# Two graph layers on one core: layer norm by sums, short reciprocals, and a second feed-forward product by seven block products

## The chip, the cores and the metric

The kernel runs on one core of a Trainium2 chip. The metric is the device time in microseconds. The engines are TensorE (PE in the profile, with its weight loads as PEld), VectorE (DVE), ScalarE (ACT), GpSimd (POOL) and SyncE (SP), which issues the transfers.

## The reference

There are 64 graphs of 256 nodes with 256 features, and an adjacency matrix for each. Two layers follow each other.

```
# layer 0
h = gat(gat(x, adj, W1, a1), adj, W2, a2)       # two graph attention layers
h = layernorm(x + h) * g_ln1 + b_ln1
ff = relu(h @ w_ff1 + b_ff1) @ w_ff2 + b_ff2    # 256 -> 1024 -> 256
x = layernorm(h + ff) * g_ln2 + b_ln2
# layer 1
attn = softmax(q k^T / sqrt(32)), 8 heads       # q, k: x @ Wq + bq, x @ Wk + bk
out = sum over r of (attn * (adj == r)) @ (x @ Wv[r] + bv[r])
x = layernorm(x + out @ Wo + bo) * g1 + beta1
ff = gelu(x @ W1 + b1) @ W2 + b2                # 256 -> 1024 -> 256
x = layernorm(x + ff) * g2 + beta2
```

All is float32.

## The kernel before

The graphs are taken in 32 pairs. `whole_way(pair)` (L943) is a Python generator that takes a pair through four stages: `gat_layers` (L515), `feed_forward` for layer 0 (L658), `attention` (L724), and `feed_forward` again for layer 1. The rows of a pair stand in one tile `x` with four row blocks, two for each graph; four such tiles exist.

The order of the instructions on each engine is written by a planner, `run` (L213), when the program is built. It has a clock for each engine, a cost in microseconds for each piece of work (`put`, L158; for matmuls `took`), the time at which a buffer or PSUM bank becomes free, and a rank. Four pairs are in flight at once, besides the generator that prepares the weights. At each step the planner takes the engine that can start earliest, and emits the first ready piece in order of rank and of the time at which it was ready. For TensorE the pair that holds the feed-forward stage stands behind the others; among the rest the oldest comes first. The order it finds is fixed by dependencies without semaphores, so each engine runs exactly this list.

*First product and projections.* The first feed-forward product and the query, key and value projections are done by seven block products instead of eight (`Second`, L344, and `Blocks`, L372): the operands' blocks are combined by additions, and the products are added up on VectorE (L392). The matmuls are at L681 (feed-forward), L754 and L759 (projections).

*Second product of a feed-forward stage.* It is done in the ordinary way. For each graph and each of its two row blocks, eight matmuls of 128 by 128 weights (the activations, `f`) and 256 moving columns (`w2`) add up in half a PSUM bank (L712), 32 matmuls for a pair. Then `add_rows` (L567) adds the bank to the rows of `x` on VectorE (L570), and `layernorm` (L572) follows for that graph, while the other graph's matmuls still run.

*Layer norm.* VectorE takes the statistics of each row block (L582, L583), adds epsilon and negates the mean (L584, L585). GpSimd raises to the power of -1/2 and multiplies by the mean (L588, L589). ScalarE normalises both row blocks (L593), VectorE multiplies by the gain and adds the shift (L598), each for both blocks in one instruction. In stages that go on, `transposed` (L608) turns the rows by VectorE, a store to memory and four gathers; in a few places at the start and the end (`hurried`, L604) TensorE transposes instead.

*Attention.* `scores(n)` (L788) is done for four combinations of graph and half of the heads. It takes four PSUM banks and multiplies queries and keys in tiles of 32 rows (L796). ScalarE takes the exponential of each head (L803), VectorE multiplies it by the adjacency (L807) and adds its halves (L811), one instruction for each head. `products(n)` (L818) multiplies with the values in tiles of 32 columns (L825) and adds the sums of the weights (L828). VectorE takes the reciprocal of those sums over 128 by 256 elements (L837), although each sum stands there 32 times, and multiplies (L838); ScalarE adds up sums and reciprocals for a check of their range (L835). The order is scores 0 and 1, products 0 and 1 together, scores 2 and 3, products 2 and 3 together.

The check of ranges decides at the end whether a second, general program has to run; with these inputs it doesn't.

Of the kernel before, what the change touches and what calls it, by code (L numbers as in the profile page):

```python
# [18 lines left out]
P = 128  # L19
# [7 lines left out]
HURRIED = 2  # L27
SLACK = 0.3
# [4 lines left out]
def two_layers(ctx: ExitStack, tc: tile.TileContext, t: dict, out: bass.AP, flag: bass.AP):  # L33
# [40 lines left out]

    rises = [const.tile([P, 2, 32], F32, name=f"rise{n}") for n in range(2)]
# [35 lines left out]
    a2, w1T = (work.tile([P, 512], F32, name="a", bufs=2 * HQ) for _ in range(2))  # L111
    junk = work.tile([P, N], F32, name="h", bufs=2 * HQ)
    w1T = w1T.rearrange("p (c m) -> p c m", c=KC)
# [27 lines left out]
    alone = {}  # L141
    free = {name: [0.0] * n for name, n in (("bank", 8), ("a", 2 * HQ), ("m", 2 * HQ), ("h", 2 * HQ), ("yb", 1), ("yT", 2), ("yTa", 1),
# [15 lines left out]
    def put(engine, us, emit, *events, rank=1, lag=0.2, kb=0, function=None, needs=None, frees=(), event=None):  # L158

        piece = {"engine": engine, "us": us, "emit": emit, "rank": rank, "lag": lag, "kb": kb, "function": function,
                 "needs": needs, "frees": frees, "event": event or Event(), "ready": 0.0, "missing": 0}
        for e in events:
            if e.time is None:
                piece["missing"] += 1
                e.then.append(piece)
            else:
                piece["ready"] = max(piece["ready"], e.time)
        if not piece["missing"]:  # L170
            waiting[engine].append(piece)
        return piece["event"]

# [39 lines left out]
    def run(besides, ways, together):  # L213
# [4 lines left out]
        together += 1  # L218
        while True:
# [23 lines left out]
            if engine == "tensor":  # L243
                sure = [n for at, n in times if at <= now - SLACK]
                g = going[min(sure, key=lambda n: (going[n][0] is besides, "ff" in (going[n][2] or ()) or alone.get("ff") is going[n][0], n))
# [11 lines left out]
            else:  # L257
                piece = waiting[engine].pop(min(able, key=lambda n: (waiting[engine][n]["rank"], waiting[engine][n]["ready"])))
# [68 lines left out]
    def first_weights(name, wide=None):  # L327
# [7 lines left out]
        return s  # L335

# [152 lines left out]
    def gat_weights(y, at, at_home, ratio, there, to, b):  # L489
# [16 lines left out]
        def scale():  # L506
            for j in range(2):
                k = 2 * b + j
                nc.scalar.activation(y[:, k, :at], y[:, k, :at], AF.Copy, scale=of["rs"][:, j:j + 1])  # L509

        there = put("vector", 1.03, lambda: weigh(0), *there, rank=b / 2, needs="e")
        there = put("vector", 1.11, lambda: weigh(1), there, rank=b / 2, frees=["rows"] * b)
        return of, put("scalar", 0.8, scale, there, rank=0)

    def gat_layers(pair, to, loads):  # L515
# [3 lines left out]
        def evacuated(to, k, wide, ps):  # L519
            return put("scalar", 0.4, lambda: nc.scalar.activation(to[:, k, :wide], ps[:, :wide], AF.Copy),  # L520
# [46 lines left out]
    def add_rows(y, p, b, *events):  # L567

        rows = y[:, of_graph(b), :].rearrange("p k d -> p (k d)")
        return put("vector", 0.6, lambda: nc.vector.tensor_tensor(rows, p, rows, ALU.add), *events, frees=["bank"])  # L570

    def layernorm(r, gb, b, *events):  # L572
        g, beta, _ = gb
        st = mv = rstd = less = None
        rows = [r[:, 2 * b + j, :] for j in range(2)]

        def statistics():
            nonlocal st, mv, rstd, less
            st, mv = small.tile([P, 2, 6], F32, name="st"), small.tile([P, 2, 2], F32, name="mv")
            rstd, less = small.tile([P, 2], F32, name="rstd"), small.tile([P, 2], F32, name="less")  # L580
            for j in range(2):
                nc.vector.bn_stats(st[:, j, :], rows[j])  # L582
                nc.vector.bn_aggr(mv[:, j, :], st[:, j, :])  # L583
            nc.vector.tensor_scalar(rstd, mv[:, :, 1], EPS, None, ALU.add)  # L584
            nc.vector.tensor_scalar(less, mv[:, :, 0], -1.0, None, ALU.mult)  # L585

        def root():
            nc.gpsimd.tensor_tensor(rstd, rstd, mhalf[:, :2], ALU.pow)  # L588
            nc.gpsimd.tensor_tensor(less, less, rstd, ALU.mult)  # L589

        def normalise():
            for j in range(2):
                nc.scalar.activation(rows[j], rows[j], AF.Identity, bias=less[:, j:j + 1], scale=rstd[:, j:j + 1])  # L593

        def scale():
            both = r[:, of_graph(b), :]
            for v, op in ((g, ALU.mult), (beta, ALU.add)):
                nc.vector.tensor_tensor(both, both, v.rearrange("p (k d) -> p k d", k=1).to_broadcast([P, 2, D]), op)  # L598

        there = put("vector", 1.22, statistics, *events)  # L600
        there = put("gpsimd", 1.2, root, there)
        return put("vector", 1.2, scale, put("scalar", 0.8, normalise, there))

# [54 lines left out]
    def feed_forward(y, normal, w, func, relieved, gb, pair, stage):  # L658

        w1, b1, w2 = w  # L660
# [3 lines left out]
        f, evacuated = [None] * NF, [[None] * NF for _ in range(2)]  # L664
# [5 lines left out]
        def slabs(t):  # L670

            rows, columns = [], (slice(0, N), slice(N, 2 * N))

            def begin():
                for c in range(2):
                    rows.append(work.tile([P, 2, 512], F32, name="ff", bufs=NF // 2))
                    for n in range(2):
                        f[t + n + c * half] = rows[c][:, n]
# [4 lines left out]
            def target(c, h):  # L683
                return rows[c][:, :, columns[h]]
# [715 lines left out]
```

## Time and profile before

| | |
|---|---|
| median of 3 runs | 3044.09 us (3042.1 to 3045.04) |
| the profiled execution, span | 3047.2 us |
| instructions in it | 52870 |
| PE busy | 2996.3 us |
| weight loads busy | 2452.5 us |
| DVE busy | 2556.8 us |
| ACT busy | 1752.5 us |
| POOL busy | 252.6 us |
| granted TensorE clock, mean | 0.995 |
| DMA queue of the data, share of 16 engines | 20.6% |

The profiled execution's own time is its span; it is 3.1 us above the median of the runs. Busy time is the time in which an engine had an instruction under way. Ends of matmuls are modelled, so their durations overlap; the distance between starts says more. In a timeline row stand the start, the length of the whole row, the engine, the line, the operation, the written and the read tiles, the tile of the array, the shape and the number of instructions; in brackets the idle time ahead of it and what ended it. In the rows of waits stand the total in microseconds, the number of times and the longest.

### The profile page before, as it was taken

The numbers are of one execution on the slowest core, as the hardware profiler recorded it, in microseconds if no ns is written. First come the engines' busy times: TensorE is split into PE (matmuls) and PEld (weight loads), VectorE is DVE, ScalarE is ACT, GpSimd is POOL, SyncE is SP. The second block draws the span as 40 slices with busy tenths as digits, with TensorE's granted clock in tenths as the row PEclk, the third lists the DMA queues.
The fourth block names the chain that finished last, engine by engine and source line by source line (L and its number), as shares of the span: only waits on it lengthen the run. The fifth ranks groups of instructions, "written<-read, shape, count | busy, mean of one in ns | idle before, by whom it ended". The sixth has DMA issues, their size and how long they took to land.

```text
span 3047.2 us, 52870 instructions
## 1 busy us (share of the span) xinstructions
PE 2996.3 (98%) x19146; PEld 2452.5 (80%) x19146; DVE 2556.8 (84%) x5993; ACT 1752.5 (58%) x4096; POOL 252.6 (8%) x518
## 2 busy tenths in 40 slices
PE   7999999999999999999999999999999999999998
PEld 6887788878888888888888888888888888788876
DVE  5888988788988888888889888889888898888875
ACT  4556666556556556555565565565555655555654
POOL 0100010001100001100001000011000011000100
PEclk8999999999999999999999999999999999999999
DMA  5211041212212222112222112221122221122100
GB/s 186 74 47 61 32 127 54 70 56 84 70 40 66 77 84 77 53 53 70 84 84 77 39 60 77 84 77 62 50 68 79 84 77 52 52 71 70 49 1 22
DMA packets 211147, 205.76 MB, mean 68 GB/s; under 512 B 22336, under 2 KB 170432, under 8 KB 210880
## 3 DMA queue, kind: packets, MB, share of 16 engines
q1 hardware_dynamic: 210464, 202.06, 20.6%
q8 instruction: 153, 2.51, 0.4%
q14 instruction: 114, 0.93, 0.1%
q10 hardware_dynamic: 416, 0.26, 0.0%
HBM read 137.51 MB, written 64.73 MB: 66 GB/s over the span
## 4 chain that ended last, share of the span: by engine, by line
PE 63%; DVE 25%; DMA 6%; ACT 2%; SPq 1%; issue 1%; POOL 0%; DVEq 0%; ACTq 0%; POOLq 0%
PE ps L712 21%; PE ps L681 15%; PE ps L825 5%; DVE x L598 4%; PE ps L759 4%; PE ps L754 4%; PE ps L544 3%; DVE h L837 3%; PE ps L796 3%; DMA home<-yb 3%; DVE st L582 2%; DVE m L807 2%; PE ps L557 2%; DMA rows<-row 2%; DVE ff L392 2%; PE ps L847 2%
## 5 line engine op out<-in xcount | busy, mean ns | idle before, releaser
L712 PE MATMUL ps<-w_L_gnn_w_ff,ff 128*128 128x256 f32 x2048 | 470.9, 381 | 0.0
L712 PE MATMUL ps<-w_L_gnn_W,ff 128*128 128x256 f32 x2048 | 456.1, 380 | 1.8 <-ACT ff L693 1.8
L593 ACT ACTIVATE x<-x,less,rstd 128x256 f32<-128x256 f32 x512 | 279.2, 596 | 294.8 <-POOL less L589 294.7
L712 PEld LDWEIGHTS ps<-w_L_gnn_w_ff,ff 128*128 128x128 f32 x2048 | 386.6, 190 | 61.5 <-issue 9.8
L712 PEld LDWEIGHTS ps<-w_L_gnn_W,ff 128*128 128x128 f32 x2048 | 388.2, 190 | 57.6 <-ACT ff L693 2.6
L588 POOL TENSOR_TENSOR rstd<-rstd,mhalf 128x2 f32<-128x2 f32 x256 | 198.3, 775 | 2765.7 <-DVE less L585 2638.0
L807 DVE TENSOR_TENSOR m<-a,adj 128x512 f32<-128x512 f32 x512 | 350.1, 684 | 57.9 <-ACT a L803 57.8
L803 ACT ACTIVATE a<-ps 128x512 f32<-128x512 f32 x512 | 268.0, 604 | 222.6 <-PE ps L796 222.5
L681 PE MATMUL ps<-yT,w_L_gnn_W1p 128*128 128x256 f32 x1280 | 315.2, 382 | 4.7 <-ACT ff L687 2.4
L392 DVE TENSOR_TENSOR ff<-ps,ff 128x512 f32<-128x512 f32 x384 | 262.7, 685 | 66.4 <-PE ps L681 58.3
L681 PE MATMUL ps<-yT,w_L_gnn_w_ff1p 128*128 128x256 f32 x1280 | 308.8, 382 | 6.8 <-ACT ff L687 5.9
L681 PEld LDWEIGHTS ps<-yT,w_L_gnn_w_ff1p 128*128 128x128 f32 x1280 | 240.6, 190 | 50.8 <-ACT ff L687 18.8
L687 ACT ACTIVATE ff<-ps 128x512 f32<-128x512 f32 x384 | 223.9, 590 | 98.4 <-PE ps L681 97.6
L681 PEld LDWEIGHTS ps<-yT,w_L_gnn_W1p 128*128 128x128 f32 x1280 | 240.2, 190 | 48.2 <-ACT ps L835 8.5
L837 DVE RECIPROCAL h<-ps 128x256 f32<-128x256 f32 x128 | 223.4, 1746 | 21.3 <-PE ps L828 20.9
L509 ACT ACTIVATE xw<-xw,rs 128x258 f32<-128x258 f32 (+1 forms) x256 | 115.9, 502 | 200.7 <-DVE rs L504 200.6
L693 ACT ACTIVATE ff<-ff,c_L_gnn_b_ff 128x256 f32<-128x256 f32 x384 | 171.6, 504 | 97.4 <-DVE ff L392 97.0
L693 ACT ACTIVATE ff<-ff,c_L_gnn_b 128x256 f32<-128x256 f32 x384 | 173.3, 501 | 85.0 <-DVE ff L392 83.8
L811 DVE TENSOR_TENSOR h<-a 128x256 f32<-128x256 f32 x512 | 213.9, 418 | 0.0
L582 DVE BATCH_NORM_STATS2 st<-x 128x6 f32<-128x256 f32 x512 | 206.0, 402 | 0.9
L570 DVE TENSOR_TENSOR x<-ps,x 128x512 f32<-128x512 f32 x256 | 170.2, 682 | 16.4 <-PE ps L712 9.3
L769 ACT ACTIVATE qk<-ps,bqk 128x256 f32<-128x256 f32 x256 | 106.6, 468 | 112.2 <-PE ps L754 111.9
(128 smaller groups left out, 5008.1 us busy)
## 6 DMA issues: line engine op xcount, KB each, us to landing
home<-yb SPq DMA_DIRECT2D x182, 256.0 KB, 2.0
yT<-home SPq DMA_DIRECT2D x728, 64.0 KB, 2.0
rows<-row SPq DMA_DIRECT2D x60, 512.0 KB, 4.0
input<-in_xT SPq DMA_DIRECT2D x32, 512.0 KB, 5.1
x<-in_x SPq DMA_DIRECT2D x32, 512.0 KB, 3.8
out<-x SPq DMA_DIRECT2D x32, 512.0 KB, 5.1
input<-in_adjT SPq DMA_DIRECT2D x30, 512.0 KB, 4.5
v<-in_adjT SPq DMA_DIRECT2D x2, 512.0 KB, 7.3
```

Of the source, the lines that this page charges most:

```text
L392: nc.vector.tensor_tensor(self.target(c, h), self.bank[bank], self.target(c, h), ALU.add)
L582: nc.vector.bn_stats(st[:, j, :], rows[j])
L588: nc.gpsimd.tensor_tensor(rstd, rstd, mhalf[:, :2], ALU.pow)
L593: nc.scalar.activation(rows[j], rows[j], AF.Identity, bias=less[:, j:j + 1], scale=rstd[:, j:j + 1])
L681: nc.tensor.matmul(to, lhsT=w1[:, a, (t + slab) * P:(t + slab + 1) * P], rhs=b, **flags)
L687: return put("scalar", 0.5, lambda: nc.scalar.activation(target(c, h), blocks.bank["x"], AF.Copy), event, rank=-1)
L693: evacuated[h][m] = put("scalar", 0.4, lambda m=m, to=to, source=source: nc.scalar.activation(to, source, func, bias=b1[:, m:m + 1]), even ...
L712: nc.tensor.matmul(p2[:, j * D:(j + 1) * D], lhsT=f[m][:, (2 * j + b) * P:(2 * j + b + 1) * P], rhs=w2[:, m, :], start=m == 0, stop=m == N ...
L803: nc.scalar.activation(a[n][o], ps[o], AF.Exp)
L807: nc.vector.tensor_tensor(m[n][o], a[n][o], adj, ALU.mult)
L811: nc.vector.tensor_tensor(h[n][o], a[n][o][:, :N], a[n][o][:, N:], ALU.add)
L837: there = put("vector", 1.68, lambda: nc.vector.reciprocal(s, po[:, N:]), there, rank=0)
```

## The change

- `layernorm` works from sums. `add_rows` adds each row block for itself with a scalar_tensor_tensor that also adds up the row, and VectorE scales the sums to negative means. ScalarE squares each block with that mean as its bias, and adds up. GpSimd scales, adds epsilon and raises to the power. VectorE does the rest in two steps for each block: add the negative mean and multiply by the gain, then multiply by the root and add the shift.
- The reciprocal of the attention's sums is taken of 128 by 8 elements: VectorE transposes blocks of 32 by 32, copies one column of each, takes the reciprocal and transposes a broadcast of it back. The check reads only these.
- Exponentials are kept for two heads in one tile; VectorE multiplies by the adjacency and adds the halves for two heads at once.
- The second product of layer 1's feed-forward (stage 2, `SEVEN`) is done by `by_seven`: seven products of 256 by 512 by 128, each of eight matmuls with 128 moving columns. Four combinations of the activations are formed in place on VectorE (1024 elements each), three combinations of the weights once at the start. Three PSUM banks take the products; VectorE adds them to quarters of the rows. When all are there, ScalarE takes the means of both graphs' rows (`means`), and the two layer norms follow. Layer 0 keeps its eight matmuls (`by_eight`).
- The planner: a pair in its second product stands behind all others, a pair in the rest of its feed-forward stage ahead of them. `together` is raised by one more, so five pairs are in flight. `put_each` lets each of several instructions of one piece be placed for itself. Scores and products alternate one at a time. Some costs are changed.

```diff
-    def layernorm(r, gb, b, *events):
+    def add_rows(y, p, b, *events):
...
+            row = y[:, 2 * b + j, :]
+            nc.vector.scalar_tensor_tensor(row, p[:, j * D:(j + 1) * D], 1.0, row, op0=ALU.mult, op1=ALU.add,
+                                           accum_out=of["less"][:, j:j + 1])
+            if j == 1:
+                nc.vector.tensor_scalar(of["less"], of["less"], -1.0 / D, None, ALU.mult)
...
+    def means(y, b, *events):
+            nc.scalar.activation(unread, y[:, 2 * b + j, :], AF.Copy, scale=-1.0 / D, accum_out=of["less"][:, j:j + 1])
...
+    def layernorm(r, gb, b, added, *events):
-                nc.vector.bn_stats(st[:, j, :], rows[j])
-                nc.vector.bn_aggr(mv[:, j, :], st[:, j, :])
-            nc.vector.tensor_scalar(rstd, mv[:, :, 1], EPS, None, ALU.add)
-            nc.vector.tensor_scalar(less, mv[:, :, 0], -1.0, None, ALU.mult)
+            nc.scalar.activation(unread, rows[j], AF.Square, bias=of["less"][:, j:j + 1], accum_out=squares[:, j:j + 1])
+            nc.gpsimd.tensor_scalar(rstd, squares, 1.0 / D, EPS, ALU.mult, ALU.add)
             nc.gpsimd.tensor_tensor(rstd, rstd, mhalf[:, :2], ALU.pow)
-            nc.gpsimd.tensor_tensor(less, less, rstd, ALU.mult)
-                nc.scalar.activation(rows[j], rows[j], AF.Identity, bias=less[:, j:j + 1], scale=rstd[:, j:j + 1])
-                nc.vector.tensor_tensor(both, both, v.rearrange("p (k d) -> p k d", k=1).to_broadcast([P, 2, D]), op)
+            nc.vector.scalar_tensor_tensor(rows[j], rows[j], of["less"][:, j:j + 1], g, op0=ALU.add, op1=ALU.mult)
+            nc.vector.scalar_tensor_tensor(rows[j], rows[j], rstd[:, j:j + 1], beta, op0=ALU.mult, op1=ALU.add)
...
+        def product(n, to, side, first=False):
+            for b in range(2):
+                for k in range(half):
+                    nc.tensor.matmul(to[:, b], lhsT=side[:, k, b * P:(b + 1) * P], rhs=w2[:, n - 1, k],
+                                     start=first and b == k == 0, stop=True, skip_group_check=True)
+            return took(1.8)
...
+        yield [w2_there, *done(0, 0)], None, 1
+        left = two_halves()
+        read4 = product(4, left[:, 0], a22, True)
+        t1 = combine(a22, a21, a22, ALU.add, *done(0, 0), *done(0, 1), read4)
+        t3 = combine(a21, a11, a21, ALU.subtract, *done(1, 1), t1)
+        yield done(1, 1), None, 1
+        x = two_halves()[:, 0]
+        read1 = product(1, x, a11, True)
+        d1 = add(quarter(0, 0), x, 0.34, read1)
+        t2 = combine(a11, a22, a11, ALU.subtract, t3, read1)
+        yield from last.p3()
+        frees_at(clock["tensor"], ["yT", "sums_yT"])
+        filling.append(alone["ff"])
+        yield [t1], None, 1
+        v = two_halves()[:, 0]
+        read5 = product(5, v, a22, True)
+        d5 = add(quarter(1, 1), v, 0.34, read5)
+        yield [t2, d1], None, 0
+        d6 = add(quarter(0, 1), x, 0.34, product(6, x, a11))
+        yield done(1, 0), None, 0
+        read2 = product(2, left[:, 1], a12)
+        d24 = add(rows[:, :, :, :P], left, 0.6, read2, read4, frees=["bank"])
+        t4 = combine(a12, a12, a11, ALU.subtract, t2, read2)
+        yield [t3, d6], None, 0
+        d7 = add(... product(7, x, a21), d5, frees=["bank"])
+        yield [t4, d5], None, 0
+        d3 = add(quarter(0, 1), v, 0.34, product(3, v, a12), frees=["bank"])
+        normal["added"] = [means(y, g, d24, d7, d3) for g in range(2)]
...
+            def invert():
+                nc.vector.transpose(s, po[:, N:])
+                nc.vector.tensor_copy(both[0][:, 1], blocks[:, :, 0])
+                nc.vector.reciprocal(both[0][:, 0], both[0][:, 1])
+                nc.vector.transpose(blocks, both[0][:, 0].rearrange("p (g i) -> p g i", i=1).to_broadcast([P, N // 32, 32]))
-            there = put("vector", 1.68, lambda: nc.vector.reciprocal(s, po[:, N:]), there, rank=0)
...
-        for n in (0, 2):
-            yield [*masked[n], *masked[n + 1], ready["v", 0, n // 2], ready["v", 1, n // 2]], None, 2
-            divided += [products(n), products(n + 1)]
-            if n == 0:
-                for later in (2, 3):
-                    yield from scores(later)
+        for n in range(4):
+            yield [*masked[n], ready["v", 0, n // 2], ready["v", 1, n // 2]], None, 1
+            divided.append(products(n))
+            if n < 2:
+                yield from scores(n + 2)
...
     def run(besides, ways, together):
         going, ways = [[besides, *next(besides)]], iter(ways)
         together += 1
+        def degree(g):
+            if g[0] in filling:
+                return 2
+            return 0 if "ff" in (g[2] or ()) or alone.get("ff") is g[0] else 1
+
+        together += 1
```

## The prediction

> **What bounds the kernel now.** I read, in this order, the busy times and the slices of the page, the table by stretches, the waits, and then timelines of TensorE, where starts count and not durations. The busy times:
>
> ```profile
> PE 2996.3 (98%) x19146; PEld 2452.5 (80%) x19146; DVE 2556.8 (84%) x5993; ACT 1752.5 (58%) x4096; POOL 252.6 (8%) x518
> ```
>
> TensorE leads. Two stretches from the middle, one period each (columns: busy us of PE, weight loads, DVE, ACT, POOL):
>
> ```profile
> 1420.00:1513.00 93.00, 92.31 (x585) 75.53 (x584) 79.25 (x187) 53.94 (x127) 7.83 (x16) 1.00 0.22 69
> 1513.00:1606.00 93.00, 93.00 (x590) 76.63 (x589) 80.48 (x189) 53.94 (x127) 7.83 (x16) 1.00 0.21 69
> ```
>
> The period of one pair of graphs is 93.2 us (L557 starts at 1428.6 and again at 1521.8); 32 periods are 2982 us of the span of 3047.2. Outside them lie about 30 us of start and a tail of 11.5 us after the last product. Inside, VectorE has 13 us of slack a period and ScalarE 39. Where does TensorE wait?
>
> ```profile
> PE ps L557 <- ACT xw L509: 9.3, 1, 9.3
> PE ps L681 <- ACT ff L687: 9.1, 18, 1.4
> ```
>
> The first is once, at the start. Waits between 300 and 2900 us sum to about 18 us. So the time is TensorE's work: its instructions times their pace. The pace comes from starts:
>
> ```profile
> 1506.30 1.89 PE L712 MATMUL ps<-w_L_gnn_w_ff,ff 128*128 128x256 f32 x8
> 1508.12 1.15 PE L796 MATMUL ps<-qk 32*128 32x256 f32 x16
> 1509.19 7.17 PE L712 MATMUL ps<-w_L_gnn_w_ff,ff 128*128 128x256 f32 x32
> 1516.30 1.07 PE L825 MATMUL ps<-a,v 128*32 128x256 f32 x16
> ...
> 1520.21 0.61 PE L828 MATMUL ps<-h,ones 128*32 128x256 f32 x8
> 1520.75 1.15 PE L796 MATMUL ps<-qk 32*128 32x256 f32 x16
> ...
> 3023.36 12.25 PE L712 MATMUL ps<-w_L_gnn_W,ff 128*128 128x256 f32 x56
> ```
>
> One matmul of the program is two records. 56 records of 256 columns in 12.25 us, less one duration of 0.38, are 0.2158 us each. And a change of tile shape costs: the first row hands over after 1.82 us, where 8 records need 1.72; L828 hands over after 0.54, where 8 records at its own pace of 0.0535 need 0.43. Over 300 to 2900 us, start to start less count times pace, the mean excess is 0.12 (0.10 to 0.14) from full-array or score tiles into or out of the 128*32 tiles of L825, 0.10 into the scores (L796), and 0.01 between full-array groups.
>
> **What the Trainium skill says.** "Perfetto Trace Analysis", section Identifying the Most-Contended Engine: busy time of matmuls is a poor measure, the busy share of weight loads a better one. The trace agrees in part: PE says 98%, but loads 80%, and the starts show that there is indeed no room. "TensorE: Matmul & The Clock Gate", section LDWEIGHTS: a load takes its columns over 1.2 GHz, 107 ns for 128. Same page, Back-to-back issue gap: at 128 columns the spacing is set by load and matmul together, 81 ns where the matmul alone is 56. The trace for float32:
>
> ```profile
> 16.87 1.06 PE L464 MATMUL ps<-ident,rise 128*128 128x128 f32 x8 [0.90 <-ACT rise L451]
> 17.76 3.41 PE L912 MATMUL ps<-c_L_gnn_b_ff2c,w_L_gnn_w_ff1p 128*128 128x1 f32 x30
> ```
>
> L912 moves one column, so it shows loads alone: (3.41 - 0.25) / 29 = 0.109 us, which agrees. L464 loads 128 columns and moves 128: (1.06 - 0.27) / 7 = 0.112, or 0.89 us to the next start over 8 = 0.111; the same group at 33.7 us gives 0.110. Load and matmul of equal length did overlap there. "Vector Engine (DVE) Microarchitecture Reference", section Points that are easy to get wrong: a scalar_tensor_tensor with two float32 sources runs at half rate. The trace does not agree: L120, such an instruction with a sum, takes 425 ns, a tensor_tensor of the same size (L811) 418.
>
> **The change part by part.**
>
> *Second product of layer two, the only part on the path.* Removed per pair: 32 matmuls of 256 columns, 64 records x 0.2158 = 13.81 us. Added: 7 products of 8 matmuls of 128 columns, 112 records. Their pace is not shown for this two-record form. Below it cannot be under the loads' 0.109; above, if a load were not hidden and took the 0.137 that L464's loads last. I take 0.1115, between L464's three readings: 12.49 us. Gain 1.32 us a pair, x 32 = 42 us (0.109: 51; 0.119: 15; 0.137: a loss of 49).
>
> *Order of the attention.* The products now come one graph half at a time, with scores between. In the order of the changed kernel, which can be listed without a run, the groups of L825 and L828 form 125 runs instead of 64. 48 more entries come from full-width work and 61 more exits, (48 + 61) x 0.12 = 13 us; the scores are entered 13 times less from there, -1. Cost 12 us.
>
> *VectorE.* By starts, a 512-element instruction takes 0.605 us, a 256-element one 0.337, one with a pointer 0.41. Off, per pair: eight row additions 4.8, eight statistics 8 x 1.5 = 12, gains and shifts 8 x 1.33 = 10.6, reciprocals 4 x 1.68 = 6.7, masks 9.7, halves 5.4: 49 us. On: twelve row additions with sums 12 x 0.45 = 5.4, their means 6 x 0.25 = 1.5, 32 centring and scaling steps x 0.41 = 13.1, four short reciprocals x 1.2 = 4.8, masks in pairs 8 x 1.14 = 9.1, halves 8 x 0.605 = 4.8, four combinations of 1024 elements x 1.14 = 4.6, additions of products 2.6: 46 us. That is 77 of 92 us instead of 80 of 93. Cost nothing on the path: it stays 15 us under TensorE. If its cover goes, each microsecond of lateness at a bank's release is one of TensorE.
>
> *ScalarE.* Off: normalising 16 x 0.545, sums of the check 8 x 0.40: 11.9. On: squares 16 x 0.545 (L693's 0.455 by starts and a read of 0.09), means 4 x 0.40, short checks 8 x 0.25, and 22 table loads more in all (93 against 71, from the order) x 1.283: 13.2. Some 55 of 92 us, hidden under TensorE; but a table load can delay the copy (L687) that TensorE waits for.
>
> *GpSimd.* The step with epsilon moves here; no row shows it. L589 (0.21) and L588 (0.78) bound it, 0 to 0.6 us more in each chain, off the path except in the tail.
>
> *Queues and order.* Five pairs are in flight instead of four, and the second product comes after all other ready work. DMA counts are the same (728 gathers, 182 stores, and so on); four loads of the last weights replace one, at the start, long before use. The seven products hold three PSUM banks for their whole length, the old two halves one at a time, while scores want four of eight. And they wait: product 3 for a combination (1.14 us) that starts only when product 2 has been read, with product 7 (1.8 us) between, 0.5 us to spare; product 7 for an addition behind product 6, with product 2 between. A mask or reciprocal of 1.1 to 1.3 us ahead in VectorE's order eats that. The row additions and L811 queue behind, and then the banks come late. Against it stands the larger stock of work. I take +3 us, from -18 (all waits go) to +32 (1 us a pair).
>
> *Tail.* From the last product to the output's issue it was 3041.6 - 3035.7 = 5.9 us, for one graph; now both graphs are normalised after it: addition 0.4, four means 1.6, four squares 2.2, GpSimd 1.0, two scalings 0.8, 0.3 of hand-overs: 6.3. Cost 0.4. At the other hurried places the chain is 1 us shorter (no statistics). Together 0.
>
> Sum against the profiled execution: 3047.2 - 42 + 12 + 3 = 3020. The median of the runs is 3.1 below the profiled time, so 3017.
>
> **The rivals.** *Loads come through* (ends slower): at 128 columns load and matmul have the same length, and one that is not fully hidden shows in each of 3584 records. It decides from 0.119 us a record on, where the 15 us of other costs eat the gain; at 0.125 the new product costs 14.0 us a pair, 6 us more over all than the old, and the sum is 3047 + 6 + 15 = 3068, 3065 in the median. For it: the skill's 81 against 56. Against: L464's 0.111. *Waits grow*: the combinations and the held banks cost 1 us a pair, 3020 + 29 = 3049, 3046 in the median, no change to be told; at 1.3 us it is slower. For it: 0.5 us to spare in an order that VectorE does not interrupt. Against: 15 us of slack and five pairs. *Waits go*: the second product fills all holes, 3020 - 21 = 2999, 2996. For it: the work in reserve; against: only 18 us are there. That the products are not fewer is excluded by the order: 1792 of 128 columns for 1024 of 256.
>
> **How the numbers follow.** The likeliest case has 0.55, loads come through 0.12, waits grow 0.18, waits go 0.15. About 0.2% (6 us) is what a measurement can tell from no change. Waits grow is split: half within it, 0.06 above; with the edge of the likeliest that gives same 0.11, slower 0.18, faster 0.71. Likeliest 3017, own range 3003 to 3032; the range reaches from 2992, with the waits gone, to 3054, the first rival at 0.122.
>
> **What would show it.** Right: the new product's records of 128 columns start 0.110 to 0.113 us apart; a period of about 92.3 us; DVE near 77 us of it; L687 still the main cause of TensorE's waits. Wrong: starts at 0.12 or more, or long idle times of TensorE before the seven products released by the combinations or their additions, or before scores for want of a bank.

## The result

The changed kernel takes 3051.78 us (median of 8 runs, 3050.32 to 3053.71); the kernel before took 3043.2 us in the runs beside it. The ratio is 1.0025, 95% interval 1.0017 to 1.0034: slower, by a little more than a measurement can hide. Predicted was 3017 us, with 3003 to 3032 as the range.

The busy times of the profile after:

```profile
PE 2980.3 (98%) x20682; PEld 2475.1 (81%) x20682; DVE 2473.2 (81%) x5869; ACT 1817.0 (60%) x4886; POOL 287.2 (9%) x518
```

The span is 3050.9 us, that is 3.7 more than before; the medians differ by 8.6, since the profiled execution of before (3047.2 us) was longer than any of its timed ones beside the experiments (spans of 3036.3 to 3046.7). VectorE has 84 us less to do than before and ScalarE 64 more; neither is the bound. Two stretches of 92.5 us from the middle (columns as before: busy us of PE, weight loads, DVE, ACT, POOL, then the granted clock, the DMA share and GB/s):

```profile
1381.00:1473.50 92.50, 89.95 (x612) 73.44 (x611) 78.98 (x188) 55.33 (x152) 10.74 (x19) 1.00 0.24 75
1473.50:1566.00 92.50, 92.37 (x627) 78.59 (x629) 68.57 (x154) 56.85 (x139) 8.10 (x12) 0.98 0.17 55
```

The period is no longer the same for each pair: it repeats after three pairs (277.4 us by the starts of the input's matmuls), 92.5 us each, where 92.3 was predicted; before, over 18 pairs, it was 92.7. The 93.2 from which the prediction counted is one pair's; from 92.7 its sums give 91.8. So the forecast of the period looks met by luck, and 0.7 us a pair are missing. TensorE's waits (total, number, longest):

```profile
PE ps L803 <- DVE ff L811: 17.0, 17, 1.9
PE ps L594 <- ACT xw L546: 11.8, 2, 8.0
...
PE ps L704 <- DVE x L652: 5.4, 2, 3.8
PE ps L732 <- ACT ff L738: 4.2, 9, 1.3
```

L803 is the new product, L811 a combination of the activations. The wait on L738, the former L687, has fallen from 9.1 to 4.2 us; L811 has taken its place with 17.0. Summed over the trace after the first 70 us, TensorE waits 38.4 us instead of 17.2. Of these, 9.2 us lie between 360 and 410 us, the second wait of L594 (3.8 us) among them. No row of the view names the scores (L924), so the want of a PSUM bank that the prediction named as a sign of being wrong was not seen there. One such hole, a place where TensorE stands still, with TensorE's timeline and VectorE's beside it:

```profile
1464.28 3.73 PE L803 MATMUL ps<-w_L_gnn_W,ff 128*128 128x128 f32 x32
1467.85 1.03 PE L732 MATMUL ps<-yT,w_L_gnn_W1p 128*128 128x256 f32 x4
1468.85 2.05 PE L803 MATMUL ps<-w_L_gnn_W,ff 128*128 128x128 f32 x16
1472.78 9.43 PE L803 MATMUL ps<-w_L_gnn_W,ff 128*128 128x128 f32 x64 [1.88 <-DVE ff L811]
1482.05 2.32 PE L732 MATMUL ps<-yT,w_L_gnn_w_ff1p 128*128 128x256 f32 x10
```

```profile
1467.58 1.22 DVE L811 TENSOR_TENSOR ff<-ff 128x1024 f32<-128x1024 f32 x1
...
1469.45 1.22 DVE L811 TENSOR_TENSOR ff<-ff 128x1024 f32<-128x1024 f32 x1
1470.58 0.68 DVE L430 TENSOR_TENSOR ff<-ps,ff 128x512 f32<-128x512 f32 x1
1471.18 0.41 DVE L397 TENSOR_TENSOR sums_yT<-yT 128x256 f32<-128x256 f32 x1
1471.51 1.22 DVE L811 TENSOR_TENSOR ff<-ff 128x1024 f32<-128x1024 f32 x1
...
1478.89 1.22 DVE L811 TENSOR_TENSOR ff<-ff 128x1024 f32<-128x1024 f32 x1
```

Three things are to be seen. The pace: 32 records in 3.73 us less one duration of 0.27 are 0.1116 us each. The chain: product 5 (x16) starts when the first combination ends (1467.58 + 1.22 = 1468.80), product 6 when the third one ends (1471.51 + 1.22 = 1472.73), and the two instructions (L430, L397) between the second and the third cost it another 0.9 us. And what comes after: the four last products are one row of 64 records because nothing else is ready; the next pair's first product (L732) begins when the last record is out, since it has to wait for the feed-forward stage, which one pair holds at a time. That row takes 9.27 us to the next start where 64 records need 7.14: product 3 waits some 0.3 us within it for the last combination (1478.89 + 1.22 = 1480.11), and the clock is down, so that the records from 1473.4 to 1476.6 us start 0.21 us apart:

```profile
1470.00:1475.00 5.00, 3.12 (x21) 2.93 (x20) 4.39 (x9) 0.91 (x2) 0.00 (x0) 0.83 0.37 110
1475.00:1480.00 5.00, 5.00 (x38) 4.84 (x36) 2.14 (x3) 0.00 (x0) 0.00 (x0) 0.83 0.11 44
```

The end of the trace has a second hole, in TensorE's timeline:

```profile
2999.55 1.89 PE L985 MATMUL ps<-w_L_gnn_Wo,qk 128*128 128x256 f32 x8
3003.00 1.17 PE L704 MATMUL ps<-ident,x 128*32 128x128 f32 x32 [1.55 <-DVE x L652]
3007.99 1.94 PE L704 MATMUL ps<-ident,x 128*32 128x128 f32 x32 [3.83 <-DVE x L652]
3010.63 5.49 PE L732 MATMUL ps<-yT,w_L_gnn_W1p 128*128 128x256 f32 x12 [0.71 <-ACT yT L708]
```

L704 are the last pair's transposes; they wait for its layer norm, and the pair before has no matmuls left to give. The last row, 12 records in 5.28 us to the next start where 2.6 are needed, runs at half the clock.

### The profile page after: what moved, and what is told of

It reads as the page before. It is cut to its first block, busy times and chain, and to the rows that moved or that the text cites. A ratio compares the mean times of both kernels' runs of the same rounds, so it can differ in the third digit from the quotient of the medians.

```text
span 3050.9 us, 56445 instructions
## 1 busy us (share of the span) xinstructions
PE 2980.3 (98%) x20682; PEld 2475.1 (81%) x20682; DVE 2473.2 (81%) x5869; ACT 1817.0 (60%) x4886; POOL 287.2 (9%) x518
## 5 line engine op out<-in xcount | busy, mean ns | idle before, releaser
L777 PE MATMUL ps<-w_L_gnn_w_ff,ff 128*128 128x256 f32 x2048 | 481.7, 383 | 0.0
L803 PEld LDWEIGHTS ps<-w_L_gnn_W,ff 128*128 128x128 f32 x3584 | 421.0, 194 | 41.7 <-DVE ff L811 24.4
L803 PE MATMUL ps<-w_L_gnn_W,ff 128*128 128x128 f32 x3584 | 433.7, 279 | 18.8 <-DVE ff L811 17.0
L777 PEld LDWEIGHTS ps<-w_L_gnn_w_ff,ff 128*128 128x128 f32 x2048 | 382.3, 190 | 77.7 <-issue 23.8
L430 DVE TENSOR_TENSOR ff<-ps,ff 128x512 f32<-128x512 f32 x384 | 262.9, 686 | 139.3 <-PE ps L732 83.8
L645 POOL TENSOR_SCALAR rstd<-squares 128x2 f32<-128x2 f32 x256 | 70.7, 276 | 2735.8 <-ACT unread L640 2735.2
L640 ACT ACTIVATE unread<-x,less 128x256 f32<-128x256 f32 x512 | 258.9, 506 | 113.2 <-DVE less L615 99.6
L732 PE MATMUL ps<-yT,w_L_gnn_W1p 128*128 128x256 f32 x1280 | 313.3, 384 | 4.7 <-ACT ff L738 4.0
L937 DVE TENSOR_TENSOR m<-a,adj 128x1024 f32<-128x1024 f32 x256 | 310.6, 1213 | 3.5 <-ACT a L933 3.5
L738 ACT ACTIVATE ff<-ps 128x512 f32<-128x512 f32 x384 | 224.3, 586 | 141.3 <-PE ps L732 136.7
L732 PE MATMUL ps<-yT,w_L_gnn_w_ff1p 128*128 128x256 f32 x1280 | 305.7, 379 | 2.2 <-DMA yT<-home 2.0
L732 PEld LDWEIGHTS ps<-yT,w_L_gnn_W1p 128*128 128x128 f32 x1280 | 239.6, 191 | 47.5 <-ACT ff L738 7.4
L732 PEld LDWEIGHTS ps<-yT,w_L_gnn_w_ff1p 128*128 128x128 f32 x1280 | 240.9, 190 | 34.6 <-issue 2.4
L646 POOL TENSOR_TENSOR rstd<-rstd,mhalf 128x2 f32<-128x2 f32 x256 | 215.8, 843 | 21.3
L612 DVE SCALAR_TENSOR_TENSOR x<-ps,x 128x256 f32<-128x256 f32 x384 | 148.8, 416 | 61.0 <-PE ps L594 44.0
L941 DVE TENSOR_TENSOR h<-a 128x512 f32<-128x512 f32 x256 | 174.9, 683 | 0.0
L887 PE MATMUL ps<-wv,yTa 128*128 128x256 f32 x640 | 167.8, 385 | 1.1 <-DVE v L903 1.1
L557 ACT ACTIVATE xw<-ps 128x260 f32<-128x260 f32 (+1 forms) x256 | 93.1, 383 | 126.5 <-PE ps L581 99.6
```

What stands on the lines that cost most here:

```text
L430: nc.vector.tensor_tensor(self.target(c, h), self.bank[bank], self.target(c, h), ALU.add)
L640: nc.scalar.activation(unread, rows[j], AF.Square, bias=of["less"][:, j:j + 1], accum_out=squares[:, j:j + 1])
L732: nc.tensor.matmul(to, lhsT=w1[:, a, (t + slab) * P:(t + slab + 1) * P], rhs=b, **flags)
L738: return put("scalar", 0.5, lambda: nc.scalar.activation(target(c, h), blocks.bank["x"], AF.Copy), event, rank=-1)
L777: nc.tensor.matmul(p2[:, j * D:(j + 1) * D], lhsT=f[c][j][:, k, g * P:(g + 1) * P], rhs=w2[:, m, :], start=m == 0, stop=m == NF - 1)
L803: nc.tensor.matmul(to[:, b], lhsT=side[:, k, b * P:(b + 1) * P], rhs=w2[:, n - 1, k], start=first and b == k == 0, stop=True, skip_group_c ...
```

## The experiments

Each kernel was timed against the kernel before, whose median was 3042.0 to 3045.3 beside them. "After" is the changed kernel, 3051.8 us.

**Which part loses?** Three parts were undone one at a time, and the products put in another order.

Run e1, the ordinary second product in layer two:

```diff
-SEVEN = (2,)
+SEVEN = ()
```

> The changed kernel with the second product of layer two done in the ordinary way again (32 matmuls of 256 columns a pair), all else as changed. Theory A: the seven products gained their 41 us of TensorE work, and some 25 us of it went back into waits of the last products for their combinations, with the slower clock after each such wait, and some 8 us into the tail. Then this run is 3052 + 41 - 33 = about 3060 us, and the tile switches of the attention (some 15 us) remain. Rival B: the waits come from the new order (five pairs, feed-forward first), whoever fills the holes. Then all 41 us come back and the time is 3085 to 3095 us.

Measured 3033.65 us, ratio to before 0.9973 (0.9963 to 0.9983): faster than both kernels, which no theory had. Its period is 92.7 us, that of before, and it hardly waits. All its waits of TensorE:

```profile
PE ps L594 <- ACT xw L546: 7.8, 1, 7.8
PE ps L130 <- DMA a<-in_L_gnn_W1T: 7.0, 1, 7.0
PE ps L581 <- ACT xw L546: 4.7, 1, 4.7
PE ps L777 <- ACT ff L744: 1.0, 4, 0.2
PE ps L502 <- ACT rise L489: 0.9, 1, 0.9
```

Only L777 is after the first 70 us. So the seven products cost 18 us in this order, although they are 41 us less work.

Run e2, the attention's products two at a time, as before:

```diff
-        for n in range(4):
-            yield [*masked[n], ...], None, 1
-            divided.append(products(n))
-            if n < 2:
-                yield from scores(n + 2)
+        for n in (0, 2):
+            yield [*masked[n], *masked[n + 1], ...], None, 2
+            divided += [products(n), products(n + 1)]
+            if n == 0:
+                for later in (2, 3):
+                    yield from scores(later)
```

> The changed kernel with the attention's products two at a time, as before the change (about 62 runs of the 32-column tiles instead of 125). Theory A: 60 fewer runs save 15 us of tile switches, 3037 us. Rival C: products taken in pairs hold more banks and wait for more masks, the waits grow by as much, 3050 us or more. Theory B expects no more than the switches, too, so this run separates A and C only.

Measured 3042.96 us (1.0001, 0.9992 to 1.001): 9 us faster than after. The direction was that of the theory with 3037; waits of 42.6 us remain.

Run e3, four pairs in flight:

```diff
-        together += 1
```

> The changed kernel with four pairs in flight instead of five. Theory A: the stock of other work only shifts the holes: 3045 to 3060 us, with the wait of L803 for the combinations as the main cause of TensorE's waits. Rival B: the fifth pair is what upsets the order; then waits fall to those of the kernel before, 3020 to 3030 us.

Measured 3062.16 us (3054.83 to 3063.4): the fifth pair is worth some 10 us. The time lies just above the range of theory A, and the main cause is not its own: TensorE waits 15.1 us for the return of transposed rows (the DMA into yT) and 6.3 for combinations.

Run e4, another order of the seven products (told in words):

```diff
-order of the products 4, 1, 5, 6, 2, 7, 3
+order of the products 4, 1, 2, 5, 6, 3, 7
```

> The changed kernel with the seven products in another order: 4, 1, 2, 5, 6, 3, 7 instead of 4, 1, 5, 6, 2, 7, 3. Product 2 needs no combination and gives VectorE 1.8 us more for the three before product 6; the combination for product 3 is then long done. Theory A: TensorE's waits of L803 for L811 (17 us) and most of the slow clock after them (about 7 us) go: 3030 us. Rival B: the holes are a want of other pairs' work; they move to other waits and the time stays at 3048 to 3056 us.

Measured 3054.03 us, as the theory said that expected the holes to move: no wait on L811 is left, but TensorE waits 39.7 us in all, now mostly for the division in the attention (L978, 15.8 us in the two largest rows that name it), masks (L937) and activations.

**Is it the chain?** Two runs take the chain away and keep the work. In e5 the combinations go to a tile that nobody reads, and the second product is therefore not the reference's:

```diff
-            return put("vector", 1.14, lambda: nc.vector.tensor_tensor(to, a, b, op), *events, rank=0)
+            return put("vector", 1.14, lambda: nc.vector.tensor_tensor(spare, a, b, op), *events, rank=0)
...
-        yield [t1], None, 1
+        yield [read4], None, 1
```

> The changed kernel, but the four combinations of the activations (1024 elements each, the same VectorE work) are written to a spare tile and no product waits for them; the products take the activations as they are, so the part of the second product that the combinations make is left out. Theory D (TensorE stands still because the seven products depend on VectorE in their middle): the waits on L811 (17 us) and the lower clock after them (about 6 us) go, 3051 - 23 = 3028, or some of it moves to the additions, up to 3040. Rival T (the loss comes from what stands around the products: both layer norms late, three banks held, the tail): 3045 to 3053, the waits under other names.

Measured 3026.9 us (0.9954, 0.9937 to 0.997), as theory D said: 25 us less than after, and a period of 91.5 us, that is 1.2 below the one with eight matmuls, as the pace promises (13.81 - 12.49 = 1.3).

In e6 the three additions in the middle of the products read a still tile besides, so the sums of products are incomplete too:

```diff
-        d1 = add(quarter(0, 0), x, 0.34, read1)
+        d1 = add(quarter(0, 0), still, 0.34, read1)
```

The two other additions are changed in the same way.

> As the one before, and besides the three additions in the middle read a still tile instead of the bank, so that none of the seven products waits for anything but its activations; the additions at the end of each bank stay, and so do the layer norms, both late, and the tail. VectorE has the same number of instructions. Left out: the combinations and three of the additions of products. Theory D: TensorE's waits are as in the kernel with eight matmuls (1 us), and the gain of 41 us in the second product is there: 3033.7 - 41 + 10 for the tail = 3003, 2995 to 3012. Rival T: 3040 or more.

Measured 3027.77 us: nothing more. The additions between the products cost nothing; the combinations are the chain. But 3003 was expected, and the time lies between both ranges. What is left stands elsewhere in the trace: waits of 11.9 us from 363 to 402 us, the longest 6.7 for the return of a pair's transposed rows (L735 on a DMA into yT), and the hole at the end as in after.

Run e7 puts the pair behind all others from its first product on:

```diff
+        filling.append(alone["ff"])
         yield [w2_there, *done(0, 0)], None, 1
...
-        filling.append(alone["ff"])
         yield [t1], None, 1
```

> The changed kernel, with the pair put behind all others from its first product of the seven on, not from the third: seven products (12.5 us) are kept in reserve instead of five (8.9 us). Nothing is left out. If the size of the reserve is what counts: the waits fall from 38 to about 25 us, 3036 to 3042. Theory D: the chain between products stays as long, and is walked through when nothing else is ready: no gain, 3048 to 3056. Rival T: the same.

Measured 3101.29 us, 50 us slower than after; all expectations missed. The two largest waits:

```profile
PE ps L803 <- DVE ff L811: 40.4, 28, 1.6
PE ps L955 <- DVE m L937: 22.7, 27, 1.1
```

Held back from its first product on, the pair starts the chain of combinations only when nothing else is ready, and TensorE then stands still at one link of it for each pair, 1.64 and 1.43 us in turn, and at the masks (L937), twice for every second one. A larger reserve is worth nothing when its work cannot run back to back.

**Is it the order?** The seven products against the eight in three more orders: products of the attention in pairs (e8, beside e2); four pairs (e11, beside e3); and the rules of order of the kernel before (four pairs, feed-forward last, products in pairs; e12 with eight and e13 with seven). What is changed in e12 is then the layer norm, the reciprocals and the masks, and besides them the costs that the planner is given, the placing of single instructions and the place of the first scores among the projections.

> The kernel with SEVEN empty (3033.7 us), with the products of the attention two at a time as in the kernel before. Some 60 changes of tile shape fewer at each pair, 15 us. If these changes are the only thing that the order of the products costs: 3017 to 3021. Rival (an order in pairs opens holes, as it did in the changed kernel, where it gave 9 us and not 15): 3023 to 3034.

> Eight matmuls in layer two (SEVEN empty) with four pairs in flight; beside it the run with seven products and four pairs (3062 us). Theory D (the products' chain costs more than they save in any order): 3040 to 3050. Theory P (the order has nothing to do with it, the seven are worth 38 us wherever the chain is covered): 3095 to 3102. Theory O (the holes of each order decide): 3030 to 3090, with waits of TensorE that account for the difference to the 92.7 us period.

> The planner and the attention's order as in the kernel before (four pairs, the feed-forward pair behind all others, products two at a time), eight matmuls in layer two; the layer norm by sums, the short reciprocals and the masks in pairs are in. If these edits are off the path, as the prediction had it: 3038 to 3046. Theory O: they change what is ready when, so the order is another, and the time is 3046 to 3100 although VectorE has less to do.

> As the one before, with the seven products in layer two. Theory P: 38 us less than that run. Theory D: 5 us less to 20 us more. Theory O: less or more by up to 40 us, as the waits of TensorE differ.

The edits are those above, and for the last two the rule of rank:

```diff
-            if g[0] in filling:
-                return 2
-            return 0 if "ff" in (g[2] or ()) or alone.get("ff") is g[0] else 1
+            return 1 if "ff" in (g[2] or ()) or alone.get("ff") is g[0] else 0
```

Medians in us:

| order | eight | seven | seven less eight |
|---|---|---|---|
| as in after | 3033.65 | 3051.78 | +18 |
| products in pairs | 3081.8 | 3042.96 | -39 |
| four pairs | 3038.56 | 3062.16 | +24 |
| rules of the kernel before | 3119.57 | 3111.6 | -8 |

The sign turns with the order. Neither "the seven are always worth 38" nor "their chain always costs more" survives. The time of e8 is far above both of its ranges, e11 and e13 lie in the range of theory O, and e12 is slower than either of its theories had it. Seven less eight, TensorE's waits after the first 70 us are +37, 0, +37 and +24 us in the four rows, and the time lost to a lower clock (half of the time at half speed) is +12, +5, +12 and 0. With the 41 us of saved work that makes +8, -36, +8 and -17: the sign of the fourth column in each row, and its size to within 3 to 16 us, which aren't placed. Ordinary matmuls have holes too, where the second product's turn comes right behind its activations; in the order in pairs with eight matmuls, the first row is

```profile
PE ps L777 <- ACT ff L744: 34.9, 17, 3.7
```

And e12, under the old rules, is 77 us slower than the kernel before, with 63 us of waits instead of 17 and 19 us lost to a lower clock instead of none. Its first row:

```profile
PE ps L774 <- ACT ff L741: 19.4, 9, 3.2
```

VectorE is less busy there than before (2317.9 us instead of 2556.8), so the waits aren't a want of VectorE's time; the order is the likely cause, and which of the edits turned it was not tried.

**Can the chain be covered?** In e9 the combinations are made early: the first goes to a tile of its own and doesn't wait for product 4, the second stays in place, and the last two take the place of operands that products 4 and 1 have read.

```diff
-        read4 = product(4, left[:, 0], a22, True)
-        t1 = combine(a22, a21, a22, ALU.add, *done(0, 0), *done(0, 1), read4)
+        t1 = combine(spare, a21, a22, ALU.add, *done(0, 0), *done(0, 1))
         t3 = combine(a21, a11, a21, ALU.subtract, *done(1, 1), t1)
+        read4 = product(4, left[:, 0], a22, True)
+        t2 = combine(a22, a11, spare, ALU.subtract, t3, read4)
...
-        t2 = combine(a11, a22, a11, ALU.subtract, t3, read1)
...
+        t4 = combine(a11, a12, a22, ALU.subtract, *done(1, 0), t2, read1)
...
-        t4 = combine(a12, a12, a11, ALU.subtract, t2, read2)
```

Products 5, 6 and 3 read the new places.

> The changed kernel with nothing left out, but the combinations of the activations are made early and not in place behind the products: the first goes to a tile of its own, the second follows at once, the third takes the place of the first operand after product 4, the fourth that of product 1's. Same VectorE work, seven products in the same order. Theory D (the chain of combinations costs 25 us, as the run with the spare tile showed): the waits on L811 are below 5 us, a period of 91.5 to 91.8, 3026 to 3032. Theory O (each change of what is ready makes another order of five pairs, with its own holes, of 0 to 1.5 us a pair, and this is worth as much as the change itself): the waits on L811 go, others come, 3032 to 3060.

Measured 3040.42 us (0.9997, 0.9988 to 1.0005), in the range of theory O. In this run the second combination has the wrong sign, so its second product isn't the reference's; the instructions are those of the right one. The wait on combinations is gone and the period is 91.5 us, but TensorE waits 13 us between 360 and 410 us and as much in the last 130 us, and the clock falls in both places.

So the last four runs ask where seven products may stand. A kept block of plain weights lets a pair choose. With e9's early combinations (signs right) e14 gives seven products to the pairs 5 to 27, e15 to 0 to 27, e17 to 2 to 28; e16 has after's combinations in place, and the pairs 4 to 27:

```diff
-        yield from (by_seven if stage in SEVEN else by_eight)(y, ...)
+        yield from (by_seven if stage in SEVEN and 5 <= pair < 28 else by_eight)(y, ...)
```

> Seven products for the pairs 5 to 27 alone, eight matmuls for the first five and the last four; combinations made early, with a tile of their own (the second one's sign set right), and one more block of plain weights kept. Nothing is left out. Theory S (the holes at the start and the end come from the seven products of the first and last pairs): no waits of TensorE over 1 us near 400 us and in the last 70 us, 3033.7 - 23 x 1.18 = 3006.5, 3002 to 3014. Rival O (another order, other holes): 3015 to 3045.

Measured 3023.57 us (0.9923, 0.9907 to 0.994). The early hole is gone, the one at the end is still there: the last pair's transposes wait 4.0 us, and the clock is at half for 10 us. The time is in the range of rival O.

> The same with seven products for the pairs 0 to 27. Theory S: the holes near 400 us are as in the run with the early combinations (some 16 us of waits, 5 of clock), those at the end go (about 15 us with the clock), the four last pairs cost 4 x 1.2 more: 3040.4 - 15 + 5 = 3030, 3025 to 3035. Rival O: the end keeps its waits, 3036 to 3045.

Measured 3032.65 us (0.995, 0.9934 to 0.9967). The time is in the range of theory S for the wrong reason in part: the early hole is back, as it said, but so is the wait of 4.0 us at the end, which it said would go.

> The changed kernel with its own combinations in place, and seven products for the pairs 4 to 27 alone. Theory S with D: the combinations still cost 1 us a pair in the middle, start and end are free of holes: 3033.7 - 24 x 0.15 = 3030, 3025 to 3035. Rival O: 3036 to 3055.

Measured 3047.41 us (1.0005, 0.9996 to 1.0013): with the combinations in place TensorE waits 17.8 us on them in 15 places, and the period is 92.5. The middle alone keeps the loss. e14 differs from this run in where and when the combinations are made, and in one pair (5 to 27 instead of 4 to 27): it takes 24 us less, waits on no combination, and has a period of 91.5. So the cost of the chain that e5 showed shows also between two kernels that leave nothing out.

> As the first of these four, with seven products for the pairs 2 to 28. Theory S: 3033.7 - 27 x 1.18 = 3002 if two pairs at the start and three at the end are enough, and up to 3018 if a hole is left there. Rival O: 3015 to 3045.

Measured 3013.0 us (0.9887, 0.9871 to 0.9904), the best of all, 32 us below before and nothing left out. It is 11 us short of theory S's 3002; 9 us more of waits than in e1 are most of that. Its waits of TensorE, the first rows:

```profile
PE ps L595 <- ACT xw L547: 9.2, 1, 9.2
PE ps L131 <- DMA a<-in_L_gnn_W1T: 7.4, 1, 7.4
PE ps L958 <- DVE m L940: 3.5, 2, 2.4
PE ps L733 <- ACT ff L739: 2.1, 8, 0.6
```

The first two are at the start of every kernel here; after 70 us it waits 10.1 us in all. Its end:

```profile
2969.98 1.08 PE L705 MATMUL ps<-ident,x 128*32 128x128 f32 x32
2970.99 1.99 PE L780 MATMUL ps<-w_L_gnn_W,ff 128*128 128x256 f32 x8
2972.91 1.08 PE L705 MATMUL ps<-ident,x 128*32 128x128 f32 x32
2973.92 1.99 PE L780 MATMUL ps<-w_L_gnn_W,ff 128*128 128x256 f32 x8
...
2989.57 12.25 PE L780 MATMUL ps<-w_L_gnn_W,ff 128*128 128x256 f32 x56
```

The last pair is back at 56 matmul records without a stop. At its transposes (L705) the pair ahead still has ordinary matmuls (L780) to give; in e14 and e15 it has none left there. Of the four kernels of this series that give the last pairs eight matmuls (e14, e15, e16 four of them, e17 three) only this one has no hole at the end, so more such pairs aren't what closes it; the phase in which the last pairs meet is the likely cause, and it wasn't tried apart. For the early hole, seven kernels with seven products from the first pair on (after, e2, e5, e6, e9, e13, e15) have waits of over 1 us between 360 and 410 us; e1, e14, e16 and e17, which give at least the first two pairs eight matmuls, have none there. But e3, e4 and e7, with seven from the first pair on in yet other orders, have none there either: eight matmuls for the first pairs close the hole in this order, but seven do not make one in every order.

## Why the prediction was wrong

**The pace held.** 0.1116 us was read from the rows, 0.1115 predicted, so 41 us of work are saved. Runs e5 and e6 show it in the period: 91.5 instead of 92.7 us. "Loads come through" was not the case.

**The order of the attention held.** Entries into and exits from the tiles of 32 columns cost 30 us of excess instead of 15.5 (100 to 3000 us, waits taken off): 15 where 12 were predicted. Undoing it gave 9 us with seven products; with eight it lost 48, with 42 us of waits instead of 1, because the order of the pairs changed with it. The price was right, but the edit cannot be had for its price.

**VectorE, ScalarE and GpSimd held as sums.** 84, 64 and 35 us over all, where 96 less, 42 more and something more were predicted; none of it shows as a bound.

**The step on queues and order failed.** It took +3 us, with -18 and +32 as the ends. Measured: waits 38.4 instead of 17.2, +21 (17.0 of the 38.4 before the new product for combinations, 9.2 between 360 and 410 us, 6.1 ahead of the end); excess at the new product's rows beyond count times pace, which holds the waits inside its rows and the lower clock, +13. That is 34, beyond its upper end. Full-array groups of 256 columns gave back 10 of their own excess. Together with -41 and +15 the terms make -2, where the spans differ by +3.7; some matmul records are missing from the traces, and the rest isn't placed.

Two readings in the step were at fault. It checked product 3 and product 7 and found 0.5 us to spare; the wait came at product 6, behind three combinations in a row, each of which starts when the one before has ended, with other instructions of VectorE queued between. Run e5 puts what this chain costs at 25 us. And it took VectorE's 15 us of slack a period, and five pairs, as cover. Slack over a period says nothing about a chain when the pair's turn comes only after everything else is used up: then the chain is all that is left, and the other pairs stand before the stage that this one holds. This is the rival "waits grow", to which 0.18 was given, with 34 / 32 = 1.1 us a pair where it was worked out with 1.

**The tail failed.** It was set to nothing on the count of instructions of the last layer norms. The loss wasn't after the last product (11.7 us to the end of the span, 11.6 before) but 30 us ahead of it: 6.1 us of waits (in the 38.4 above), and a lower clock for 10 us. The prediction had said of these "other hurried places" that the chain is 1 us shorter. In the kernel before, the ordinary second product of the pair ahead stood there, 16 records in front of the first transposes and 16 between the two groups:

```profile
2998.18 3.62 PE L712 MATMUL ps<-w_L_gnn_W,ff 128*128 128x256 f32 x16
3001.78 1.08 PE L649 MATMUL ps<-ident,x 128*32 128x128 f32 x32
3002.79 3.72 PE L712 MATMUL ps<-w_L_gnn_W,ff 128*128 128x256 f32 x16
3007.20 1.08 PE L649 MATMUL ps<-ident,x 128*32 128x128 f32 x32 [0.69 <-DVE x L598]
```

**The row of holes was read from one side.** The prediction counted 18 us of waits in before, between 300 and 2900 us, as what could be gained. (The trace has 17.2 us after the first 70, and 12.6 of them between 300 and 2900.) Run e1 shows that nearly all of it can be had without the seven products (waits of 1.0 us; 8 us in the time, with the tile changes still in), by the other edits together; and e12 that the same norms, reciprocals and masks under the old rules cost 77. Neither was foreseen.

## What to carry to other kernels

When one stage is held by one pair at a time and its last part is kept as filler, that part must run back to back once it is all there is: make its operands early, into a tile of their own, before its turn, and prefer a plain product over a cheaper one that stops halfway. Price a saving per unit of work by the period it gives when nothing waits, and the holes apart, at the start, in the middle and at the end. Where a planner writes the order, an edit off the path can move the time by more than the edit on it (here from -39 to +24 for the same saving), so try it under two or three orders before judging it, and mix the variants where few units are in flight.

## What the runs showed of the hardware

The granted clock fell after shorter waits than expected. The Trainium skill, "TensorE: Matmul & The Clock Gate", section HAM oscillation — how this bites in real kernels, gives gaps of over about 3.4 us as those after which the clock goes down. Here it fell after some waits of 1.88 us: 0.83 in both stretches of 5 us about the one at 1472.78, and 0.66 in the 5 us after the one at 1644.72 in e16, which is half speed for 3.4 us. After others of the same length it did not, and none of e7's 28 waits on combinations of up to 1.64 us lowered it. The waits near 3.8 us in after both did. A wait of 1.9 us can therefore cost 3.6 us, half of the 3.4 us being lost besides. Nor does it take one long wait: in e6 the clock was 0.66 from 385 to 390 us, after two waits of 0.97 and 1.11 us (up to 384.28 and 386.02).
